# Message passing on sorted buckets: more groups scattered in pairs, column heads fetched sooner, other buffer counts

## The chip, the cores and the metric

The kernel runs on one core of one Trainium2 chip. Its time is the device time of one execution in microseconds (us). Three runs of the kernel before are given, and one profiled execution, whose trace shows every instruction of the five engines: PE (matrix products), DVE (vector operations), ACT (activations), POOL (here it issues the indirect DMAs) and SP (it issues the plain DMAs).

## The reference

There are 12,500 nodes with 128 features each and 400,000 edges, each with a source `src`, a destination `dst`, 20 attributes `f` and a weight. The edges are sorted by `dst`, while `src` is random.

```python
h   = relu(layernorm(x))
hh  = h @ W_in2f.T
Wij = (smu(f_ij @ W_f1.T + b_f1) @ W_f2.T + b_f2) * rcut_ij[:, None]
x_ij = hh[dst] * Wij
agg = segment_sum(x_ij, src, 12500)
out = x + smu(agg @ W_o1.T + b_o1) @ W_o2.T + b_o2
```

Here `smu` is a smooth bend that the kernel computes with a Gelu and a linear part. Each edge makes a message of 128 numbers, and the messages are summed by `src`, which comes in no order.

## The kernel before

**Tiles, groups, epochs.** The edges form 3125 tiles of 128. Four tiles are a *group* (782 of them), two groups a *super-group*. The 391 super-groups are divided into ten *epochs* (`PARTS`). The nodes are divided into 98 *bins* of 128.

**Scatter.** For each edge of a group the kernel computes the bin of its source and its rank among the edges of the epoch that fall into this bin (`mark_bins`, `bins`, `count`, `read`, `number`: one-hot marks, prefix sums on PE, a maximum on DVE). That gives a row number in a buffer in device memory with a fixed number of rows per bin and epoch (`CAP`). POOL then sends the group's message tile there with indirect DMAs (`scatter_rows`, L1069), one for each tile of 128 rows. A row has 129 numbers: the message and the place of the source in its bin. Three buffers are used in turn by the epochs.

**Sum.** In the epoch that follows, SP reads the buffer back (`fetch`, four chunks ahead), DVE turns the places into one-hot matrices `se` (`choose`, L1117), and PE multiplies rows by them and sums over a bin (`add`, L1130). DVE adds the result of four bins at a time to `agg` (L1144). `chores` and `parts` spread this work evenly over the groups of the epoch.

**The order.** All of PE, DVE, ACT and SP is written out by hand in one loop over positions `p` (L1637). At each position the steps of several groups are issued: the sends of this group, the products of the next, the gathers of the one after, the counts of the next but one. `seq` is the order of the groups. The groups of the last two epochs (23 super-groups, `s >= EARLY`) are interleaved into epochs 1 to 4: they are computed early, already multiplied by the first output weight, and stored in `kept_rows`; their bins are counted at that time too. They are scattered only in the *last stretch*, after epoch 7 (L1819 to L1851), where `refill` reads them back four groups ahead through SP.

**Pairs.** In some groups, tiles 2 and 3 are sent together with tiles 0 and 1. Rows of the two halves that have the same bin are put side by side, so that one indirect DMA writes two rows per partition. A paired group needs two sends in place of four, and one tile of *leftovers* (rows that found no partner) is sent as a fifth tile by a later group, its *host*. For this PE turns the keys of the group (`spread_keys`, L813), DVE compares them (`match`, L822, with the number of matches added up in `met`), PE ranks the rows without a partner (`rank_left`, L832), DVE builds the placing matrix (`place_left`, L839), PE permutes (`permute`, L859), ACT takes the result out (`take_pairs`, L870 and L871; leftovers go into `lt`, three buffers), and DVE makes the leftovers' bins (`number_left`, L849). The host counts them as one tile more (L707, L708, L750, L804). Which group is paired is decided in L539 to L550: after `EVERY` positions since the last pair (4 in epoch 0, 3 in the others), from position 80 on, and not in the last ten groups of an epoch; a group at least five positions behind a pair becomes its host. The host is looked for first. In the last stretch, every third group (`LATE_EVERY`) is paired, and its leftovers are sent by themselves three groups later.

**Column heads.** The columns `dst` and `src` are read in seven heads of 512 tiles (`head_of`). Their steps stand in a timetable in *slots* (three per position). `fetched` issues the two loads on SP, and `based`, DVE's first use (L410), comes 2.5 slots later; for heads whose time is before `known` (the first three of the six in the timetable) the loads are moved 9 slots forward (L1443).

**Buffers.** Messages `ms` rotate through nine buffers, halves `cd` through two, the rows read back `rw` through four.

Of the kernel before, what the change touches and what calls it, by code (L numbers as in the profile page):

```python
# [20 lines left out]
P = 128  # L21
# [10 lines left out]
WIN = 42  # L32
PARTS = (60, 58, 58, 58, 47, 37, 27, 23, 16, 7)
EVERY = (4, 3, 3, 3, 3, 3, 3, 3)
UNPAIRED = 10
MOST_PAIRS = 224
FIRST_PAIRED = 80
LATE_EVERY = 3
WIDER = 0.17
SENT_LAST = 2  # L40
BUFS = 3
SIGMA = 4.95
ROW = P + 1
# [7 lines left out]
def gnn_kernel(  # L51
# [46 lines left out]
    for a, n in eps_of:  # L98
        last_groups = UNPAIRED / (SUP // GRP)
        paired = n - last_groups if 0 < len(CAP) < len(eps_of) - 1 else 0  # L100
        if not CAP:
            paired = max(0, n - last_groups - FIRST_PAIRED / (SUP // GRP))
        every = LATE_EVERY if len(CAP) >= len(eps_of) - SENT_LAST else EVERY[len(CAP)]
# [241 lines left out]
    with tc.tile_pool(name="ld", bufs=4) as ld, \  # L345
            tc.tile_pool(name="edge", bufs=2) as edge, \
            tc.tile_pool(name="cnt", bufs=3) as cnt, \
            tc.tile_pool(name="msg", bufs=9) as msg, \
            tc.tile_pool(name="row", bufs=4) as rowp, \
# [116 lines left out]
        dsf, ssf = front[:, 2, :FEW], front[:, 3, :FEW]  # L466
        met = const.tile([P, 2 * MOST_PAIRS], F16, name="met")
        h_first = met.bitcast(BF)[:, :3 * D].rearrange("p (b k d) -> p b k d", b=1, k=3)
        nc.scalar.dma_start(x_sb[:, 0:1, :], bin_rows(x, 0, 1))
# [69 lines left out]
        for p, g in enumerate(seq):  # L539
            if g // PER >= EARLY:  # L540
                continue
            since_pair += 1
            if wanting and p >= wanting[0][0] + 5:
                host[g] = wanting.pop(0)[1]
                assert epoch[g // PER] == epoch[host[g] // PER]
            elif (since_pair >= (math.floor, math.ceil)[len(paired) % 2](EVERY[epoch[g // PER]])
                  and (epoch[g // PER] or p >= FIRST_PAIRED) and seq[p - 1] // PER < EARLY and g + UNPAIRED < ends_of[epoch[g // PER]]):
                paired[g] = len(paired)
                wanting.append((p, g))
                since_pair = 0  # L550
        assert not wanting
# [3 lines left out]
        assert 2 * len(pair_no) <= met.shape[1]  # L555
        late_keys = const.tile([P, len(late_pairs), GRP], F32, name="late_keys")
        so_end = const.tile([P, NB], F16, name="so_end")
# [251 lines left out]
        def spread_keys(g):  # L809

            kt = ps1.tile([P, GRP * P], F32, name="pt")
            for j in range(2):
                nc.tensor.transpose(kt[:, j * P:(j + 1) * P], keys_of[g][:, j:j + 1].to_broadcast([P, P]), ident)  # L813
            matched[g] = kt

        def match(g):

            kt, key = matched[g], keys_of.pop(g)
            pp = edge.tile([P, 6 * P], F32, name="mt", bufs=2)
            o = 2 * pair_no[g]  # L820
            for i in range(2):
                nc.vector.scalar_tensor_tensor(pp[:, i * 2 * P:(i + 1) * 2 * P].rearrange("p (j e) -> p j e", j=2),  # L822
                                               kt[:, :2 * P].rearrange("p (j e) -> p j e", j=2), key[:, 2 + i:3 + i],
                                               onesb.unsqueeze(1).to_broadcast([P, 2, P]),
                                               op0=ALU.is_equal, op1=ALU.mult, accum_out=met[:, o + i:o + i + 1])
            matched[g] = (kt, pp)

        def rank_left(g):

            kt, i = matched[g][0], 2 * pair_no[g]  # L830
            at_ = kt[:, 2 * P:2 * P + 2]
            nc.tensor.matmul(at_, tri, met[:, i:i + 2], start=True, stop=False, skip_group_check=True)  # L832
            nc.tensor.matmul(at_[:, 1:2], ones_h, met[:, i:i + 1], start=False, stop=True, skip_group_check=True)

# [16 lines left out]
        def permute(g):  # L851
# [9 lines left out]
            matched[g] = po  # L861

        def take_pairs(g):
# [546 lines left out]
        def due(t, f):  # L1410
            timetable.append((t, len(timetable), f))
# [361 lines left out]
        def flag_formed():  # L1773

            few_met = ps1.tile([P, GRP * P], F32, name="pc")[:, :2 * len(pair_no)]
            nc.tensor.matmul(few_met, ones_h, met[:, :2 * len(pair_no)], start=True, stop=True)
            sums = mv.rearrange("p b s -> p (b s)")[:, :len(pair_no)]
            nc.vector.tensor_reduce(sums, few_met.rearrange("p (g i) -> p g i", i=2), op=ALU.add, axis=AX.X)
            least_met = const.tile([P, 1], F32, name="least_met")
            nc.vector.tensor_reduce(least_met, sums, op=ALU.min, axis=AX.X)  # L1780
            i = 4 + 2 * EPOCHS
# [292 lines left out]
```

## Time and profile before

| | |
|---|---|
| runs shown | 3869.15, 3873.28, 3874.53 us (median 3873.28) |
| profiled execution | 3877.55 us, its span 3875.5 us |
| PE, DVE, ACT, POOL busy | 85%, 79%, 73%, 75% of the span |
| mean busy share of the 16 DMA engines | 63.4% for SP's queue, 17.6% for POOL's |
| memory traffic | 904.79 MB, mean 233 GB/s |

How to read the rows: a group's row gives the line of the kernel, the engine, the operation, out<-in by the program's names, the shapes and the count; then the busy time in us and the mean of one in ns; then the idle time of the engine just before these instructions, with what ended most of it. A row of waits names the engine and line that waited, what for, the total in us, how often, and the longest. A row of the timeline begins with the start and the duration in us. A row of a window gives its bounds and length, then the busy time (and the number) for PE, weight load, DVE, ACT, POOL, and the granted clock, DMA share and GB/s; where it was asked for one line's instructions, only the engine of that line is shown. The busy share of PE is that of matmuls whose ends are modelled.

The epochs can be told apart in the trace by counting the message products (L1002 and L992, one per group that is not kept): epoch 1 begins at about 618 us, epoch 2 at 1202, epoch 3 at 1750, epoch 4 at 2305, epoch 5 at 2750, epoch 6 at 3094, epoch 7 at 3365, and the last stretch at about 3566. POOL's last send begins at 3815.7 us.

### The profile page before, as it was taken

To read this page: it belongs to the slowest core of one execution; us is meant where nothing else is said; L and a number is where in the kernel's file an instruction comes from. 1 tells how busy PE (TensorE), PEld (TensorE's weight loads), DVE (VectorE), ACT (ScalarE), POOL (GpSimd) and SP (SyncE) were. 2 spreads that over 40 slices of the span, in tenths; PEclk is the share of its full clock that TensorE was granted. 3 is DMA by queue.
4 is the path that set the end of the run, shared out by engine and by line. 5 is a ranking of instruction groups with operands and counts; after the bars stand their busy time and mean duration, and the time that the engine had idled before them with its cause. 6 is when DMAs were issued, how large, how long until landed. Compare 5 with 4: busy or idle time off the path is not lost.

```text
span 3875.5 us, 89505 instructions
## 1 busy us (share of the span) xinstructions
PE 3289.4 (85%) x27505; PEld 2851.7 (74%) x27505; DVE 3066.3 (79%) x8171; ACT 2831.6 (73%) x8043; POOL 2889.8 (75%) x2977
## 2 busy tenths in 40 slices
PE   8766677888888888899888889899989988999667
PEld 4345555777777777788777778788888878888557
DVE  7887786778777888888888888888888877888557
ACT  7776666778777888788888888788877876776102
POOL 6777777777677777777777777777777777777776
PEclk9988898999999999999999999999999999999889
DMA  5887878889897877788887878878888888887988
GB/s 155 225 238 222 235 222 236 243 242 257 249 264 222 230 220 222 225 238 230 227 225 221 239 213 249 235 230 234 246 234 237 245 233 226 237 237 213 285 258 241
DMA packets 663934, 904.79 MB, mean 233 GB/s; under 512 B 180372, under 2 KB 463128, under 8 KB 663322
## 3 DMA queue, kind: packets, MB, share of 16 engines
q1 hardware_dynamic: 556025, 666.99, 63.4%
q0 software_dynamic: 100112, 219.73, 17.6%
q10 hardware_dynamic: 7312, 12.29, 0.9%
q8 instruction: 223, 3.65, 0.4%
q14 instruction: 262, 2.14, 0.2%
HBM read 500.66 MB, written 398.03 MB: 232 GB/s over the span
## 4 chain that ended last, share of the span: by engine, by line
PE 31%; DVE 17%; DMA 17%; issue 8%; ACT 8%; POOL 7%; SPq 1%; DVEq 0%; ACTq 0%; POOLq 0%
DMA buf<-ms,ix 11%; PE pg L1130 10%; POOL buf L1072 7%; PE pw L970 6%; PE pt L859 5%; PE pc L735 3%; ACT hg L945 3%; DVE se L1117 3%; DVE pc L779 2%; DMA rbc<-rel_dram 2%; DVE mt L822 2%; DVE ms L1002 2%; PE ph L926 2%; DVE eo L654 2%; DMA buf<-lt,ix 2%
## 5 line engine op out<-in xcount | busy, mean ns | idle before, releaser
L1072 POOL DMA_INDIRECT buf<-ms,ix x2578 | 2506.5, 972 | 846.6 <-issue 566.1
L1130 PE MATMUL pg<-se,rw 128*128 128x128 f32 x8036 | 1171.4, 285 | 116.6 <-DVE se L1117 52.7
L1130 PEld LDWEIGHTS pg<-se,rw 128*128 128x128 f32 x8036 | 1042.0, 195 | 162.6 <-DVE agg L1144 56.6
L945 ACT ACTIVATE hg<-ph,w_sb 128x128 f32<-128x128 f32 x2784 | 788.6, 364 | 491.3 <-PE ph L926 468.0
L970 PE MATMUL pw<-w_f,ge 128*128 128x128 f32 x5568 | 778.3, 284 | 12.7 <-DVE ms L1002 7.6
L970 PEld LDWEIGHTS pw<-w_f,ge 128*128 128x128 f32 x5568 | 701.1, 197 | 31.1 <-ACT ge L898 8.0
L1117 DVE TENSOR_TENSOR se<-irow_ps,rw 128x1536 f32<-128x1536 f32 (+1 forms) x345 | 587.4, 1703 | 94.3 <-DMA rw<-buf 74.6
L779 DVE TENSOR_REDUCE pc<-pc 128x4 f32<-128x392 f32 (+1 forms) x782 | 463.6, 593 | 154.5 <-PE pc L735 150.4
L617 ACT ACTIVATE oh<-rbc,nrow 128x512 bf16<-128x512 uint8 x724 | 538.2, 743 | 38.9 <-DMA rbc<-rel_dram 38.9
L618 ACT ACTIVATE oh<-oh,onesb 128x512 bf16<-128x512 bf16 x742 | 535.3, 721 | 24.2
L1002 DVE TENSOR_TENSOR ms<-pw,hg 128x512 f32<-128x512 f32 x513 | 351.4, 685 | 128.5 <-PE pw L972 42.6
L859 PE MATMUL pt<-cd,mt 128*128 128x129 f32 (+1 forms) x2304 | 311.2, 287 | 82.4 <-DVE at L839 76.1
L735 PE MATMUL pc<-eo,tri 128*128 128x392 f16 x782 | 266.9, 341 | 110.2 <-DVE ix L801 88.4
L859 PEld LDWEIGHTS pt<-cd,mt 128*128 128x128 f32 x2304 | 286.5, 199 | 96.5 <-issue 49.6
L926 PE MATMUL ph<-hw,oh 126*128 126x128 bf16 x2784 | 280.7, 224 | 24.0 <-ACT hg L945 24.0
L898 ACT ACTIVATE ge<-pu 128x512 f32<-128x512 f32 x452 | 275.6, 610 | 18.7 <-PE pu L890 16.7
L735 PE MATMUL pc<-so,ones_h 128*128 128x392 f16 (+1 forms) x965 | 281.4, 314 | 0.0
L972 PE MATMUL pw<-wls,f 128*128 128x128 bf16 x2784 | 273.7, 222 | 0.0
L735 PEld LDWEIGHTS <-ones_h 128*128 128x128 f16 x1554 | 154.9, 100 | 149.1 <-issue 32.7
L926 PEld LDWEIGHTS <-oh 126*128 126x128 bf16 x2784 | 220.0, 100 | 45.6 <-issue 28.1
L654 DVE TENSOR_TENSOR eo<-irow_ps,ed 128x784 f16<-128x784 f16 x391 | 218.2, 558 | 37.2 <-ACT ed L644 34.2
L1072 POOL DMA_INDIRECT buf<-lt,ix x192 | 185.9, 968 | 65.5 <-issue 28.7
(339 smaller groups left out, 5088.7 us busy)
## 6 DMA issues: line engine op xcount, KB each, us to landing
rw<-buf SPq DMA_DIRECT2D x292, 774.0 KB
f<-f_parts SPq DMA_DIRECT2D x370, 240.0 KB
buf<-zero SPq DMA_DIRECT2D x146, 387.0 KB
rbc<-rel_dram SPq DMA_DIRECT2D x389, 128.0 KB
buf<-ms,ix POOLq DMA_INDIRECT x2578
f_parts<-hs SPq DMA_DIRECT2D x104, 360.0 KB
rw<-buf SPq DMA_DIRECT2D x49, 645.0 KB
f_parts<-hs SPq DMA_DIRECT2D x106, 240.0 KB
```

The lines of the kernel that those rows point to most:

```text
L617: nc.scalar.activation(oh, loaded[s][1][:, o:o + n], AF.Abs, bias=pneg if s < FEW // SUP else nrow)
L618: nc.scalar.activation(oh, oh, AF.Relu, scale=-1.0, bias=onesb[:, 0:1])
L735: nc.tensor.matmul(to, by, of, start=start, stop=stop, skip_group_check=True)
L779: nc.vector.tensor_reduce(sl[:, :n], pc[:, :n], op=ALU.max, axis=AX.X)
L859: nc.tensor.matmul(po[:, j * (ROW + 1):j * (ROW + 1) + w], pp[:, o:o + P], cd[:, i, :w], start=(i == 0), stop=(i == 1))
L926: nc.tensor.matmul(ph[:, j * P:(j + 1) * P], oh[:3 * WIN, a:a + P], hw[:3 * WIN, g % PER, :], start=True, stop=True)
L945: nc.scalar.activation(hg[:, j * P:(j + 1) * P], rows_of[g][:, j * P:(j + 1) * P], AF.Copy, scale=w_sb[:, t + j:t + j + 1])
L970: nc.tensor.matmul(pw[:, a:a + P], ge[:, a:a + P], w_f2, start=(a == 0), stop=False, skip_group_check=True)
L1002: nc.vector.tensor_tensor(ms[:, :n, 0:P], pw.rearrange("p (j f) -> p j f", f=P)[:, :n], hg.rearrange("p (j f) -> p j f", f=P)[:, :n], op=A ...
L1072: i = nc.gpsimd.indirect_dma_start(out=(wide if g in host or g in pair_no else bufs)[k][:, :], out_offset=bass.IndirectOffsetOnAxis(ap=ix, ...
L1117: nc.vector.tensor_tensor(se[:, a:a + n], own.unsqueeze(1).to_broadcast([P, n, P]), rows_in[c][:, a:a + n, P:P + 1].to_broadcast([P, n, P] ...
L1130: nc.tensor.matmul(pgs[0][:, g, :], rows_in[c][:, o, 0:P], sel[c][:, o, :], start=(q == 0), stop=(q == Q[k] - 1))
```

## The change

- **More pairs.** The distance is 3 in epoch 0 and, in the others, 2 and 3 in turn (`EVERY` 2.5, rounded down and up alternately); pairs begin at position 50; a pair is looked for before a host, so that hosts come at a distance of 5 to 8. In the last stretch two groups of three are paired. `SIGMA` is 4.6, and epoch 0 has 59 super-groups and epoch 7 has 24; the bucket sizes `CAP` come out as before. The sums of matches no longer fit into `met` alone and go on in the unused `down`; `late_keys` lies in `mv`.
- **Destinations sooner.** The loads of all six heads in the timetable are moved 9 slots forward.
- **Six buffers for leftovers.** `lt` has six buffers; messages `ms` have eight in place of nine. Late leftovers lie in two `ge` tiles, late halves `cd` in part in `oh`. There are four spill places per buffer instead of two.
- **Kept rows five groups ahead.** `refill` runs five groups ahead in place of four. In the last stretch keys are turned in another bank (`pw`), and `place_of_left` comes before `number_left`.

```diff
-PARTS = (60, 58, 58, 58, 47, 37, 27, 23, 16, 7)
-EVERY = (4, 3, 3, 3, 3, 3, 3, 3)
+PARTS = (59, 58, 58, 58, 47, 37, 27, 24, 16, 7)
+EVERY = (3,) + (2.5,) * 7
-FIRST_PAIRED = 80
-LATE_EVERY = 3
+FIRST_PAIRED = 50
+LATE_OF = 2, 3
+LATE_FREE = 6
-SIGMA = 4.95
+SIGMA = 4.6
...
-    SPILLS = 2
+    SPILLS = 4
...
-            tc.tile_pool(name="msg", bufs=9) as msg, \
+            tc.tile_pool(name="msg", bufs=8) as msg, \
...
-            if wanting and p >= wanting[0][0] + 5:
-                host[g] = wanting.pop(0)[1]
-            elif (since_pair >= (math.floor, math.ceil)[len(paired) % 2](EVERY[epoch[g // PER]])
+            if (since_pair >= (math.floor, math.ceil)[len(paired) % 2](EVERY[k]) and (k or p >= FIRST_PAIRED)
+                    and seq[p - 1] // PER < EARLY and g + UNPAIRED < ends_of[k]):
                 paired[g] = len(paired)
                 wanting.append((p, g))
                 since_pair = 0
+            elif wanting and p >= wanting[0][0] + 5:
+                host[g] = wanting.pop(0)[1]
...
-        late_pairs = list(range(EARLY * PER + LATE_EVERY - 1, LATE_END - 3, LATE_EVERY))
+        late_pairs = [g for g in range(EARLY * PER + 2, LATE_END - 3) if (g - EARLY * PER) % LATE_OF[1] >= LATE_OF[1] - LATE_OF[0]]
...
-            kt = ps1.tile([P, GRP * P], F32, name="pt")
+            kt = ps1.tile([P, GRP * P], F32, name="pt" if g in paired else "pw")
...
-            lt = cnt.tile([P, ROW + 1], F32, name="lt", bufs=3)
+            lt = cnt.tile([P, ROW + 1], F32, name="lt", bufs=6) if g in paired else late_left(g)
...
-            due(t + 0.5 - (SOONER if t < known else 0), stages.pop(0))
+            due(t + 0.5 - SOONER, stages.pop(0))
...
-                    cd = apart_of[g] = msg.tile([P, 2, ROW + 1], F32, name="cd", bufs=2)
+                    if late_pairs.index(g) % 5 < 3:
+                        cd = edge.tile([P, SUP * P], BF, name="oh", bufs=3).bitcast(F32)[:, :2 * (ROW + 1)]
+                        cd = apart_of[g] = cd.rearrange("p (j r) -> p j r", j=2)
+                    else:
+                        cd = apart_of[g] = msg.tile([P, 2, ROW + 1], F32, name="cd", bufs=2)
...
-            few_met = ps1.tile([P, GRP * P], F32, name="pc")[:, :2 * len(pair_no)]
-            nc.tensor.matmul(few_met, ones_h, met[:, :2 * len(pair_no)], start=True, stop=True)
-            nc.vector.tensor_reduce(sums, few_met.rearrange("p (g i) -> p g i", i=2), op=ALU.add, axis=AX.X)
+            for a, b, at_ in ((0, n, met), (n, len(pair_no), more_met)):
+                by_pair = at_[:, :2 * (b - a)].rearrange("p (g i) -> p g i", i=2)
+                for i in range(2):
+                    nc.tensor.matmul(few_met[:, a:b], ones_h, by_pair[:, :, i], start=(i == 0), stop=(i == 1))
...
-        for g in range(g1, g1 + 4):
+        AHEAD_OF = 5
+        for g in range(g1, g1 + AHEAD_OF):
             refill(g)
...
-            refill(g + 4)
+            refill(g + AHEAD_OF)
...
+            if g - 1 in late_pairs:
+                place_of_left(g - 1)
             if g in late_pairs:
                 number_left(g)
                 count_left(g)
             parts(hi)
-            if g - 1 in late_pairs:
-                place_of_left(g - 1)
```

More of the change, by code (lines that the diff above doesn't have):

```diff
@@ L102, in gnn_kernel @@
             paired = max(0, n - last_groups - FIRST_PAIRED / (SUP // GRP))
-        every = LATE_EVERY if len(CAP) >= len(eps_of) - SENT_LAST else EVERY[len(CAP)]
+        late_one = len(CAP) >= len(eps_of) - SENT_LAST
+        every = LATE_OF[1] / LATE_OF[0] if late_one else EVERY[len(CAP)]
+        if late_one and paired:
+            paired = n - LATE_FREE / (SUP // GRP)
         mean = (n + WIDER * paired / every) * SUP * P * P / N
@@ L466, in gnn_kernel @@
         dsf, ssf = front[:, 2, :FEW], front[:, 3, :FEW]
[L467 to L468 removed]
+        met = const.tile([P, 3 * D], F16, name="met")
+        h_first = met.bitcast(BF).rearrange("p (b k d) -> p b k d", b=1, k=3)
         nc.scalar.dma_start(x_sb[:, 0:1, :], bin_rows(x, 0, 1))
@@ L542, in gnn_kernel @@
             since_pair += 1
-            if wanting and p >= wanting[0][0] + 5:
-                host[g] = wanting.pop(0)[1]
-                assert epoch[g // PER] == epoch[host[g] // PER]
-            elif (since_pair >= (math.floor, math.ceil)[len(paired) % 2](EVERY[epoch[g // PER]])
-                  and (epoch[g // PER] or p >= FIRST_PAIRED) and seq[p - 1] // PER < EARLY and g + UNPAIRED < ends_of[epoch[g // PER]]):
+            k = epoch[g // PER]
+            if (since_pair >= (math.floor, math.ceil)[len(paired) % 2](EVERY[k]) and (k or p >= FIRST_PAIRED)
+                    and seq[p - 1] // PER < EARLY and g + UNPAIRED < ends_of[k]):
                 paired[g] = len(paired)
@@ L824, in match @@
                                                onesb.unsqueeze(1).to_broadcast([P, 2, P]),
[L825 removed]
+                                               op0=ALU.is_equal, op1=ALU.mult, accum_out=met_of(g, i))
             matched[g] = (kt, pp)
         def rank_left(g):
[L830 removed]
+            kt = matched[g][0]
             at_ = kt[:, 2 * P:2 * P + 2]
[L832 to L833 removed]
+            nc.tensor.matmul(at_, tri, met_of(g, 0, 2), start=True, stop=False, skip_group_check=True)
+            nc.tensor.matmul(at_[:, 1:2], ones_h, met_of(g, 0), start=False, stop=True, skip_group_check=True)
         def place_left(g):
```

26 lines of the change are left out of this document (20 added, 6 removed).

## The prediction

> **What bounds the kernel now.** I read the page's busy times first. No engine looks full there, POOL least of all, so I took POOL's rows and then its instructions in order of time:
>
> ```profile
> span 3875.5 us, 89505 instructions
> PE 3289.4 (85%) x27505; PEld 2851.7 (74%) x27505; DVE 3066.3 (79%) x8171; ACT 2831.6 (73%) x8043; POOL 2889.8 (75%) x2977
> L1072 POOL DMA_INDIRECT buf<-ms,ix x2578 | 2506.5, 972 | 846.6 <-issue 566.1
> L1072 POOL DMA_INDIRECT buf<-lt,ix x192 | 185.9, 968 | 65.5 <-issue 28.7
> L1072 POOL DMA_INDIRECT buf<-ms,ix_kept x163 | 156.7, 962 | 49.7 <-issue 46.0 <-DMA buf<-ms,ix_kept 1.8 <-DMA hic<-in_x 0.3
> 3499.18 0.96 POOL L1072 DMA_INDIRECT buf<-lt,ix  x1 [0.30 <-issue]
> 3500.44 0.96 POOL L1072 DMA_INDIRECT buf<-ms,ix  x1 [0.30 <-issue]
> ```
>
> A send occupies POOL for 0.96 us and is followed by 0.30 us in which nothing is waited for: one per 1.26 us, whether it carries one row per partition (lt) or two. The three rows hold 2933 sends, 3705 us at 1.263 each, while their busy and idle time together are 3811 us. POOL is 97% full with sends; about 105 us are starvation. It is not starved everywhere:
>
> ```profile
> L1072 POOL DMA_INDIRECT buf<-ms,ix x695 | 676.7, 974 | 244.0 <-issue 164.9 <-ACT ms L1052 20.6 <-ACT hg L945 14.1
> L1072 POOL DMA_INDIRECT buf<-lt,ix x63 | 61.2, 971 | 19.6 <-issue 10.4 <-DVE ms L992 1.5 <-DVE pc L779 1.2
> ...
> L1072 POOL DMA_INDIRECT buf<-ms,ix x289 | 279.2, 966 | 88.2 <-issue 61.3 <-DMA buf<-ms,ix 4.6 <-ACT oh L617 3.1
> L1072 POOL DMA_INDIRECT buf<-lt,ix x27 | 26.1, 967 | 8.2 <-issue 2.7 <-DVE so L701 0.9 <-DVE ix L801 0.6
> ```
>
> The first two rows are 700 to 1700 us (epochs 1 and 2): 1001.5 us for 758 sends, 1.32 each. The last two are 1800 to 2200 us (epoch 3): 401.7 for 316, 1.27 each. So in epochs 1 and 2 POOL runs out of work now and then: PE, DVE and ACT, which make the messages, are no faster than POOL. I call them the makers. How far they are ahead at the end of epoch 7:
>
> ```profile
> 3565.85 0.68 DVE L1002 TENSOR_TENSOR ms<-pw,hg 128x512 f32<-128x512 f32 x1
> ...
> 3599.18 0.96 POOL L1072 DMA_INDIRECT buf<-ms,ix_kept  x1 [0.30 <-issue]
> ```
>
> The last message of epoch 7 is made at 3566.5; POOL begins the kept rows at 3599.2, so that message's four sends began at 3594.1: a reserve of 27.6 us. Both sides bind, in turn. A pair relieves POOL by one send and loads the makers; which weighs more decides.
>
> **What a pair costs the makers.** Walking the pairing rule through the order of groups gives, for epochs 0 to 7, 8, 34, 33, 33, 27, 21, 15 and 12 pairs now (183) and 19, 42, 41, 41, 33, 25, 18 and 15 after (234); in the last stretch 9 become 17. That is 59 sends fewer, 74.5 us of POOL. Each early pair adds, beside a plain group (its host's extra work included):
>
> ```profile
> L822 DVE SCALAR_TENSOR_TENSOR mt<-pt,key,onesb 128x256 f32<-128x256 f32 x366 | 161.7, 479 | 21.1 <-PE pt L813 19.9
> L840 DVE TENSOR_TENSOR mt<-irow_ps,at 128x256 f32<-128x256 f32 x192 | 81.5, 424 | 6.6
> L707 DVE TENSOR_SCALAR el<-mv,lat 128x98 f16<-128x98 f32 x183 | 53.8, 294 | 0.3
> L708 DVE TENSOR_TENSOR so<-so,el 128x98 f16<-128x98 f16 x183 | 39.0, 213 | 6.3
> L859 PE MATMUL pt<-cd,mt 128*128 128x129 f32 (+1 forms) x2304 | 311.2, 287 | 82.4 <-DVE at L839 76.1
> ```
>
> DVE: two of the first row (0.96) and one of each of the next three (0.93), 1.9 us, and, as an estimate from these, some 0.7 for four or five smaller ones: 2.6. PE: 311.2/192 = 1.6 us of permuting and under 1 us of turning and counting. Some of this falls into idle time, so the price is better measured. The last ten groups of an epoch have no pairs. In the same windows I counted L654 (one per two groups) and L840 (one per pair); epoch 2 first, then epoch 5, L654 ahead of L840 in each:
>
> ```profile
> 1215.00:1695.00 480.00, 30.73 (x55) 0.98 0.79 225
> 1695.00:1750.00 55.00, 3.92 (x7) 0.97 0.85 236
> 1215.00:1695.00 480.00, 13.15 (x31) 0.98 0.79 225
> 1695.00:1750.00 55.00, 0.42 (x1) 0.97 0.85 236
> ...
> 2760.00:3036.00 276.00, 15.69 (x28) 0.98 0.84 233
> 3036.00:3094.00 58.00, 3.90 (x7) 1.00 0.92 257
> 2760.00:3036.00 276.00, 8.06 (x19) 0.98 0.84 233
> 3036.00:3094.00 58.00, 0.42 (x1) 1.00 0.92 257
> ...
> 3390.00:3520.00 130.00, 7.83 (x14) 0.97 0.87 239
> 3530.00:3565.00 35.00, 2.23 (x4) 1.00 0.75 207
> 3390.00:3520.00 130.00, 3.82 (x9) 0.97 0.87 239
> 3530.00:3565.00 35.00, 0.00 (x0) 1.00 0.75 207
> ```
>
> With a for a group and c for a pair: epoch 2, 110a + 31c = 480 and 14a + c = 55, so c = 2.07; epoch 5, 56a + 19c = 276 and 14a + c = 58, so c = 2.93; epoch 7, 28a + 9c = 130 and 8a = 35, so c = 0.83. I take 2.07, since 24 of the 51 new early pairs lie in epochs 1 to 3, which resemble epoch 2, and keep 0.83 and 2.93 as ends. 51 × 2.07 = +106 us for the makers (42 to 149).
>
> The Trainium skill (Perfetto Trace Analysis, Identifying the Most-Contended Engine) judges TensorE's headroom by weight-load share, not matmul share; the page of the profile has 74% against 85%. By it the pair's PE work would find more room than I grant, and c would go to its low end, the first rival below.
>
> **Destinations sooner.** Between 320 and 500 us:
>
> ```profile
> DVE base_i L410 <- DMA rw<-in_dst_col: 37.9, 3, 15.0
> POOL buf L1072 <- DVE ix L804: 6.9, 1, 6.9
> ```
>
> The fourth to sixth column heads are fetched 2.5 slots before use; now 11.5. Three slots make a group, so the two loads of each head go onto SP's queue three groups sooner, ahead of the loads of edges, destinations and windows that those groups issue. Three groups are 618/120 × 3 = 15 us, the longest of the waits. I take 35 of the 37.9 away (0 to 38). The head takes an rw buffer of four that much sooner; if it isn't free, SP waits and every load behind it is late.
>
> **Buffers.** The makers' waits for places that POOL still holds:
>
> ```profile
> ACT lt L871 <- DMA buf<-lt,ix: 17.7, 11, 5.6
> ACT ms L1052 <- DMA buf<-ms,ix: 10.3, 6, 6.2
> ACT ms L1050 <- DMA buf<-ms,ix: 5.9, 7, 1.6
> DVE ms L1002 <- DMA buf<-ms,ix: 21.1, 21, 2.5
> ```
>
> Six leftover buffers end the first (17.7); the others (37.3) shrink because POOL, with fewer sends, frees messages sooner. Eight message buffers in place of nine work against that by one group, four sends, 5 us of reserve. I take all 55 away (0 to 55).
>
> **Costs of nothing.** Hosts yield to pairs and come at a distance of six mostly: the leftover has longer to land its count, same instructions. The sums of met need four small matmuls for one and one DVE reduction fewer, while PE waits for epoch 8's rows. Late leftovers lie in ge, late halves in oh: both unused there until the output begins, after POOL's last send; late keys are turned in bank pw, free there too. place_of_left goes ahead of number_left on DVE, two short operations:
>
> ```profile
> 3565.00:3817.00 252.00, 171.92 (x1306) 153.71 (x1305) 148.65 (x235) 21.02 (x50) 191.21 (x199) 0.88 0.83 264
> DVE se L1117 <- DMA rw<-buf: 61.2, 13, 26.2
> SPq L1771 <- DMA buf<-ms,ix_kept: 11.9, 5, 3.5
> ...
> L1536 DVE TENSOR_SCALAR drow<-pcol 128x1 f32<-128x1 f32 x20 | 1.3, 138 | 0.0
> ```
>
> In the last stretch DVE is busy 149 of 252 us and PE 172, each with waits for rows still in flight, which cover eight more late pairs (8 × 5 us over all engines). Without that cover they cost up to 8 × 2.07 = 17. Reading kept rows five groups ahead with eight buffers makes SP wait for the sends of three groups back rather than five; the row fetches for the sums queue behind that wait and DVE waits for those. They are asked for four chunks ahead, so I put it at 0, with the 11.9 above once more as the upper end. Four spill places per epoch instead of two repeat the 20 operations of the last row: 1.3 us at most, in epoch 0 before the makers have anything to catch up. Bucket sizes come out the same, so reads and clears stay; one super-group moves from epoch 0 to 7 with its work. A pair writes 640 rows for 512, in fewer sends, beside the other transfers.
>
> **The sum.** The makers' end of epoch 7 moves by −35 + 106 − 55 = +16, to 3582. The reserve was 27.6; fed by the ten unpaired groups alone, (4 × 1.263 − 3.85) × 10 = 12 us (a is 3.78 from epoch 2's equations, 3.93 from epoch 5's) and a start near 1, it becomes 13. So POOL ends epoch 7 at +16 − 15 = +1. The last stretch is POOL's: 8 × 1.263 = −10. The 59 us after the last send stay. Together −9: the profiled run (3877.55 us, 2 more than its span) would be 3868; the median of the runs shown, 3873.28, lies 4 below it, so 3864.
>
> **Rivals.**
> - *The pairs' work fits into idle time.* c at 0.83 takes 51 × 1.24 = 63 off: 3801; POOL alone allows 3873 − 74.5 = 3799, so some 3805. For it: PE, DVE and ACT each idle 15 to 27%. Against: epoch 2's and 5's rows.
> - *The pairs cost the makers 2.93 each* (slower). Place: the chain of turning keys (PE), matching (DVE), ranking (PE), placing (DVE) and permuting (PE), which at a distance of two uses the one bank pt in every group. Price 51 × 0.86 = +44: 3908. It decides from c = 2.07 + 9/51 = 2.25 on. For it: PE's 76.1 us of waits for at above; against: epochs 0 to 3, where most pairs go, have fewer sums per group.
> - *Destinations sooner does not do what it says:* the loads wait for something other than their place. +35: 3899. Against: the waits are the only ones of their kind, the first three heads already go sooner and have none.
> - *DVE sets the time by its share.* If DVE stayed at its 79%, 59 × 2.6 = 153 us more would be 194 us more: 4067. Against: POOL's spacing. The section of the Trainium skill named above ranks DVE, ACT and POOL by occupancy; by that rule DVE (79%) would be the most contended, ahead of POOL (75%); POOL's 1.26 us spacing does not agree.
>
> **Chances.** Forecast 0.44 (its own range 3840 to 3890), the rivals 0.22, 0.23, 0.08, 0.03. A measurement here can tell 0.2%, 8 us, from no change. Faster: 0.24 of the forecast, 0.22, 0.02 of the second rival, 0.48. Same: 0.11, 0.04 and 0.02, 0.17. Slower: 0.35. The range runs from near POOL's floor, 3805, to 3902, most of the second rival.
>
> **What would show it.** Right: the three waits at L410 gone; waits for lt gone; 2874 sends, still 1.26 us apart where fed; POOL's idle time beyond 0.30 per send up from 105 us towards 150 in epochs 1 to 6, with PE and DVE busier there; the reserve at the end of epoch 7 about halved. The first rival would show as idle time that does not grow; the second as longer waits at L859 and its neighbours and a later end of epoch 7. What would make me wrong most: a price per pair away from 2.07.

## The result and the profile after

The changed kernel takes 3926.68 us (median of four runs, 3924.54 to 3929.99) against 3872.11 us (3869.15 to 3874.53) before: ratio 1.0142 with a 95% interval of 1.0124 to 1.0160. It is slower by some 55 us, where 3864 us was forecast, and it lies outside the range of 3805 to 3902. The profiled executions, on which the working below rests, are 47 us apart: 3924.54 us (span 3922.8) and 3877.55 us (span 3875.5).

The page of the kernel after: the span, the busy times, and POOL's rows (count | busy, mean ns | idle before, and what ended it).

```profile
span 3922.8 us, 92185 instructions
PE 3349.1 (85%) x28254; PEld 2939.6 (75%) x28570; DVE 3178.1 (81%) x8771; ACT 2888.3 (74%) x8332; POOL 2841.5 (72%) x2918
L1095 POOL DMA_INDIRECT buf<-ms,ix x2476 | 2412.6, 974 | 847.0 <-issue 576.4 <-DMA buf<-ms,ix 37.9 <-ACT ms L1075 29.0
L1095 POOL DMA_INDIRECT buf<-lt,ix x234 | 227.8, 974 | 141.3 <-DVE ix L816 84.3 <-issue 22.0 <-DVE eo L666 5.2
L1095 POOL DMA_INDIRECT buf<-ms,ix_kept x147 | 143.7, 978 | 63.0 <-issue 42.6 <-ACT ge L894 12.4 <-DMA ms<-kept_rows 4.5
L1095 POOL DMA_INDIRECT buf<-ge,ix x17 | 16.7, 982 | 5.9 <-issue 3.4 <-DVE lat L860 0.9 <-DVE ix L1845 0.7
```

The 2874 sends that were worked out are there (2476 + 234 + 147 + 17), each still 0.97 us long with 0.30 behind it. POOL works 48 us less than before. But it waits more: the time between the beginnings of two sends, as far as it exceeds 1.30 us, adds up to 202 us after and 91 before. For epoch 0, epochs 1 to 4, epochs 5 to 7 and the last stretch, in this order, it is 28, 149, 4 and 21 us after, and 27, 57, 7 and 0.5 before. The largest new wait is for the index of a host's fifth send. Its rows among the waits (engine, line, what for: total in us, times, longest), after and then before:

```profile
POOL buf L1095 <- DVE ix L816: 88.6, 61, 5.1
```

```profile
POOL buf L1072 <- DVE ix L804: 11.9, 16, 6.9
```

POOL sends a host's leftovers ahead of the host's own messages, and their index is made shortly before those messages. So the wait says that POOL has nothing else left to send: it has caught up with the makers, 61 times for 16.

Where the time went is read from POOL's sends by stretch. The stretches begin with the first send of epoch 1, the first of epoch 5 and the first kept row. Columns: bounds, length, POOL's busy time and sends, clock, DMA share, GB/s. After:

```profile
622.00:2817.00 2195.00, 1568.54 (x1612) 0.97 0.80 230
2817.00:3634.70 817.70, 621.96 (x642) 0.98 0.83 234
3634.70:3864.00 229.30, 160.40 (x164) 0.91 0.90 272
```

Before:

```profile
644.00:2778.00 2134.00, 1592.54 (x1642) 0.97 0.83 235
2778.00:3599.10 821.10, 624.82 (x644) 0.96 0.82 230
3599.10:3817.00 217.90, 165.37 (x172) 0.89 0.89 285
```

- **Epochs 1 to 4**: 30 sends fewer, 61 us longer. Per send 1.362 us after and 1.300 before. POOL is starved here: the makers set the time. Since epoch 1 begins 22 us sooner, epoch 5 begins 39 us later.
- **Epochs 5 to 7**: two sends fewer (ten more pairs, and one super-group with eight sends more), 3.4 us shorter. Per send 1.274 and 1.275 us. POOL sets the time here, in both kernels.
- **Last stretch**: eight sends fewer, 11.4 us longer. Per send 1.398 and 1.267 us: POOL is starved where it was not.

39 − 3.4 + 11.4 = 47 us, which is the whole difference of the spans. So the pairs cost time exactly where POOL was already waiting, and the sends that they save count only in epochs 5 to 7, where there are few of them.

The makers' side of epochs 1 to 4, epoch by epoch: the windows go from the first message of an epoch to the first of the next, with busy time and count of PE, weight load, DVE, ACT and POOL. After:

```profile
606.00:1200.00 594.00, 499.46 (x4285) 445.82 (x4339) 450.70 (x1281) 467.03 (x1382) 412.21 (x424) 0.95 0.85 243
1755.00:2332.00 577.00, 506.12 (x4405) 451.68 (x4463) 470.38 (x1316) 477.88 (x1370) 420.12 (x433) 0.98 0.78 221
2332.00:2790.00 458.00, 417.25 (x3733) 379.38 (x3779) 391.28 (x1064) 374.44 (x1078) 326.29 (x336) 0.99 0.80 230
```

Before, the same three epochs (1, 3 and 4):

```profile
618.00:1202.00 584.00, 492.72 (x4194) 433.38 (x4193) 434.83 (x1202) 460.11 (x1340) 427.93 (x441) 0.94 0.87 248
1750.00:2305.00 555.00, 495.52 (x4318) 437.12 (x4317) 454.31 (x1236) 469.34 (x1329) 421.97 (x437) 0.98 0.80 227
2305.00:2750.00 445.00, 407.80 (x3663) 366.99 (x3661) 379.31 (x1002) 367.73 (x1042) 333.29 (x345) 0.99 0.83 237
```

With eight, eight and six pairs more, these epochs take 10, 22 and 13 us longer; epoch 2, with eight more, takes 7 longer. Over the four it is 52 us for 30 pairs, 1.7 each. DVE's busy time grows by 16, 16 and 12 us, PE's by 7, 11 and 9.

The reserve at the end of epoch 7, from the last message (DVE) and the first kept send (POOL), kernel after:

```profile
3598.16 0.68 DVE L1025 TENSOR_TENSOR ms<-pw,hg 128x512 f32<-128x512 f32 x1
...
3634.73 0.96 POOL L1095 DMA_INDIRECT buf<-ms,ix_kept  x1 [0.30 <-issue]
```

The message is made at 3598.8, its four sends began at 3634.7 − 4 × 1.26 = 3629.7: 30.8 us, against 27.6 before. It was not halved.

### The profile page after: what moved, and what is told of

Same layout as the page of the kernel before. It is cut to its first block, busy times and chain, and to the rows that moved or that the text cites. A ratio compares the mean times of both kernels' runs of the same rounds, so it can differ in the third digit from the quotient of the medians.

```text
span 3922.8 us, 92185 instructions
## 1 busy us (share of the span) xinstructions
PE 3349.1 (85%) x28254; PEld 2939.6 (75%) x28570; DVE 3178.1 (81%) x8771; ACT 2888.3 (74%) x8332; POOL 2841.5 (72%) x2918
## 3 DMA queue, kind: packets, MB, share of 16 engines
q0 software_dynamic: 100112, 223.62, 17.7%
## 5 line engine op out<-in xcount | busy, mean ns | idle before, releaser
L1095 POOL DMA_INDIRECT buf<-ms,ix x2476 | 2412.6, 974 | 847.0 <-issue 576.4
L630 ACT ACTIVATE oh<-oh,onesb 128x512 bf16<-128x512 bf16 x743 | 536.0, 721 | 24.1
L870 PE MATMUL pt<-cd,mt 128*128 128x129 f32 (+1 forms) x2880 | 373.8, 280 | 55.5 <-DVE at L850 49.7
L1025 DVE TENSOR_TENSOR ms<-pw,hg 128x512 f32<-128x512 f32 x462 | 316.3, 685 | 111.8 <-PE pw L995 36.2
L870 PEld LDWEIGHTS pt<-cd,mt 128*128 128x128 f32 x2880 | 346.4, 194 | 67.3 <-issue 38.8
L1095 POOL DMA_INDIRECT buf<-lt,ix x234 | 227.8, 974 | 141.3 <-DVE ix L816 84.3
L833 DVE SCALAR_TENSOR_TENSOR mt<-pt,key,onesb 128x256 f32<-128x256 f32 x468 | 207.0, 480 | 52.1 <-PE pt L825 49.6
```

What stands on the lines that cost most here:

```text
L630: nc.scalar.activation(oh, oh, AF.Relu, scale=-1.0, bias=onesb[:, 0:1])
L870: nc.tensor.matmul(po[:, j * (ROW + 1):j * (ROW + 1) + w], pp[:, o:o + P], cd[:, i, :w], start=(i == 0), stop=(i == 1))
L1025: nc.vector.tensor_tensor(ms[:, :n, 0:P], pw.rearrange("p (j f) -> p j f", f=P)[:, :n], hg.rearrange("p (j f) -> p j f", f=P)[:, :n], op=A ...
L1095: i = nc.gpsimd.indirect_dma_start(out=(wide if g in host or g in pair_no else bufs)[k][:, :], out_offset=bass.IndirectOffsetOnAxis(ap=ix, ...
```

## Experiments

A ratio is always to the kernel before, run on the same chip. On three of the chips the kernel before took 5914 to 5979 us instead of 3865 to 3872; their runs are told apart, at the end.

**Old distances in the changed kernel.** The pairs of the epochs go back to 189 (133 in place of 157 in epochs 1 to 4); everything else of the change stays.

```diff
-EVERY = (3,) + (2.5,) * 7
-FIRST_PAIRED = 50
+EVERY = (4,) + (3,) * 7
+FIRST_PAIRED = 80
```

> The changed kernel with the old pairing of epochs 0 to 7 alone (distance 4 in epoch 0 from position 80, 3 elsewhere; 183 early pairs), all else as changed. If the added early pairs cost the makers about 2 us each in epochs 1 to 4 (theory), POOL begins the last stretch about 35 us sooner than the changed kernel's 3635 us, and the time is 3880 to 3895. If the eight message buffers are the cause (rival), the time stays above 3910 and the reserve at the ends of the epochs stays lower than before.

Measured: 3899.40 us, ratio 1.0093 (1.0077 to 1.0110), about 19 us better than the change as a whole. That is 4 us above what the theory allowed and well below the rival's 3910. POOL begins the last stretch at 3608, 27 us sooner. The makers take 2151 us for epochs 1 to 4 where the changed kernel takes 2184: 33 us for 24 pairs, 1.4 each. Most of the way back to the kernel before is still missing.

**Late thirds in the changed kernel.** One group of three is paired in the last stretch, as before.

```diff
-LATE_OF = 2, 3
+LATE_OF = 1, 3
```

> The changed kernel with every third group paired in the last stretch as before (9 late pairs, not 17), all else as changed. If the late pairs at two of three make POOL wait in the last stretch (theory), POOL's waits of 2 to 4 us between 3680 and 3760 us go, the stretch of 229 us falls to about 217, and the time is 3910 to 3917. If reading five groups ahead with eight buffers makes POOL wait (rival), the waits stay and the time is 3927 or more.

Measured: 3918.30 us, ratio 1.0135 (1.0118 to 1.0152), which isn't told apart from 1.0142. The trace says more. POOL's rows from 3638 to 3858 us of this kernel, its last stretch:

```profile
L1095 POOL DMA_INDIRECT buf<-ms,ix_kept x163 | 158.4, 972 | 49.7 <-issue 44.8 <-DMA buf<-ms,ix_kept 3.0 <-ACT ge L894 0.6
L1095 POOL DMA_INDIRECT buf<-ge,ix x9 | 8.9, 987 | 2.7 <-issue 1.8 <-ACT agg L1181 0.6 <-ACT oh L1795 0.3
```

172 sends in 219.4 us, 1.28 each; with two of three, 164 in 229. The waits for L894 (a late leftover taken out by ACT) fall from 12.4 us to 0.6. So the eight additional late pairs lose some 10 us instead of gaining 10, and reading five groups ahead hardly makes POOL wait.

**Both at once.**

```diff
-EVERY = (3,) + (2.5,) * 7
-FIRST_PAIRED = 50
-LATE_OF = 2, 3
+EVERY = (4,) + (3,) * 7
+FIRST_PAIRED = 80
+LATE_OF = 1, 3
```

> Both undone: old pairing everywhere; what remains of the change is the sooner column loads, six leftover buffers, eight message buffers and kept rows read five groups ahead. Theory: the two effects add, 3865 to 3880, no slower than the kernel before. Rival (buffers): 3895 or more.

Measured: 3890.26 us, ratio 1.0057 (1.0038 to 1.0075). Beside the kernel with old distances alone this is 9 us better, the last stretch 220 us instead of 226; so the late thirds do show in the time here. Beside the one with late thirds alone it is 28 us better: that is what the added early pairs cost. The two effects do add, but the time lies between the theory's 3880 and the rival's 3895. With the pairs nearly those of before, the kernel is still 0.57% slower than before.

**Destinations sooner, alone**, in the kernel before.

```diff
-            due(t + 0.5 - (SOONER if t < known else 0), stages.pop(0))
+            due(t + 0.5 - SOONER, stages.pop(0))
```

> The kernel before with the sooner column loads alone. The three waits at L410 (37.9 us) go. Theory: epoch 1's first message comes some 25 us sooner but POOL, which still has its sends, lets only 5 to 10 us of it through: 3862 to 3868. Rival (the makers set the time throughout): 3840 to 3850. Second rival (an rw buffer that is not free makes SP wait): 3872 or more.

Measured: 3863.12 us, ratio 0.9993 (0.9984 to 1.0003). Waits of this kernel between 300 and 604 us (engine, line, what for: total, times, longest), and one of the whole trace:

```profile
ACT oh L617 <- DMA rbc<-rel_dram: 48.7, 20, 6.8
...
DVE base_i L410 <- DMA rw<-in_dst_col: 1.6, 1, 1.6
```

The answering rows of the kernel before, 300 to 618 us:

```profile
DVE base_i L410 <- DMA rw<-in_dst_col: 37.9, 3, 15.0
ACT oh L617 <- DMA rbc<-rel_dram: 20.8, 8, 6.1
```

The waits for the column heads go, as the change means it. But the loads of relative destinations, behind the heads on SP's queue or beside them, are now waited for 28 us longer. The makers begin epoch 1 at 603.5 instead of 618.3, POOL at 637 instead of 644: of 37.9 us, 15 reach the makers and 7 reach POOL, and no difference in the time can be measured. Part of that may be the difference from one execution to another: the kernel of the next experiment, whose heads are those of before and are waited for 38.1 us, begins epoch 1 at 609.1.

**Eight message buffers, alone**, in the kernel before.

```diff
-            tc.tile_pool(name="msg", bufs=9) as msg, \
+            tc.tile_pool(name="msg", bufs=8) as msg, \
```

> The kernel before with eight message buffers, again, since on the chip of the first try PE stood still so often that the kernel before took 5979 us. Theory: the ninth message buffer was worth 0.4 to 0.7% (15 to 27 us). Rival (what was left of the loss without the added pairs comes from the order of pairs and hosts): within 0.15% of the kernel before.

Measured: 3868.97 us, ratio 1.0000 (0.9989 to 1.0011). In the kernel before, the ninth buffer is worth nothing that can be measured.

**Old pairs, with the old buffers as well** (nine for messages, three for leftovers, in the kernel "both").

```diff
-            tc.tile_pool(name="msg", bufs=8) as msg, \
+            tc.tile_pool(name="msg", bufs=9) as msg, \
...
-            lt = cnt.tile([P, ROW + 1], F32, name="lt", bufs=6) if g in paired else late_left(g)
+            lt = cnt.tile([P, ROW + 1], F32, name="lt", bufs=3) if g in paired else late_left(g)
```

> The changed kernel with old pairing, nine message and three leftover buffers, again. Theory (the message buffer): within 0.15% of the kernel before. Rival (the order of pairs and hosts): still 0.4% slower or more.

Measured: 3885.14 us, ratio 1.0043 (1.0029 to 1.0057), not to be told from 1.0057. The buffers are not what remains, or at most a small part of it. POOL's stretches in this kernel and, behind them, in the one with destinations sooner alone (epochs 1 to 4, then 5 to 7):

```profile
628.00:2764.00 2136.00, 1585.85 (x1635) 0.97 0.83 234
2764.00:3592.00 828.00, 629.34 (x651) 0.97 0.81 230
```

```profile
637.00:2761.00 2124.00, 1598.17 (x1641) 0.97 0.82 235
2761.00:3581.70 820.70, 624.05 (x644) 0.97 0.81 230
```

The super-group moved to epoch 7 is seven more sends and 7.3 us in POOL's stretch. Epoch 0, one super-group shorter, gives 9 us back to POOL and 9 to the makers; but in epochs 1 to 4 it is 12 us longer, with six more pairs there (hosts yield to pairs). That would fit 1.8 to 2 us a pair; it is read off one execution of each (3872.99 us, the shortest of its six, and 3861.73), and no run has the moved super-group or the order of hosts alone on a chip of the usual speed. So the 17 to 22 us that remain are not settled: of some 55 us, the added early pairs explain 28 and the late ones 9.

**Fewer pairs where the makers set the time.** In the kernel before with destinations sooner: every 3.5 groups in epochs 1 to 4, 113 pairs there for 127.

```diff
-EVERY = (4, 3, 3, 3, 3, 3, 3, 3)
+EVERY = (4, 3.5, 3.5, 3.5, 3.5, 3, 3, 3)
```

> The kernel before with sooner columns and pairs at distances of 3 and 4 in turn in epochs 1 to 4, again. On the chip with the slow PE this was 2.5% faster than the kernel before, as it must be where the makers set the time. Here: 10 to 25 us faster than the kernel before if the makers set the time in epochs 1 to 4; 15 to 25 us slower if POOL does; both in turn: 3 to 15 us slower.

Measured: 3860.61 us, ratio 0.9984 (0.9974 to 0.9993): the opposite edit to the change, and slightly faster than the kernel before. It is 7 us, in none of the three ranges that were expected, and it is not told apart from destinations sooner alone (0.9993, 0.9984 to 1.0003). POOL's stretch of epochs 1 to 4:

```profile
636.00:2760.00 2124.00, 1608.87 (x1657) 0.97 0.83 235
```

That is 16 sends more than with destinations sooner alone, in the same 2124 us. POOL's idle time beyond 1.30 us per send is 56 us, the least so far.

**The same with six leftover buffers and eight for messages**, and a distance of 2.5 in epochs 5 to 7.

```diff
-EVERY = (4, 3, 3, 3, 3, 3, 3, 3)
+EVERY = (4, 3.5, 3.5, 3.5, 3.5, 2.5, 2.5, 2.5)
-SIGMA = 4.95
+SIGMA = 4.6
-            tc.tile_pool(name="msg", bufs=9) as msg, \
+            tc.tile_pool(name="msg", bufs=8) as msg, \
-            lt = cnt.tile([P, ROW + 1], F32, name="lt", bufs=3)
+            lt = cnt.tile([P, ROW + 1], F32, name="lt", bufs=6)
```

> The same, and pairs at distances of 2 and 3 in turn in epochs 5 to 7, with six leftover and eight message buffers. In the changed kernel POOL had a reserve of 19 to 31 us at the ends of these epochs, so the makers can carry more pairs there. Theory: 10 pairs fewer sends in a stretch that POOL sets, 12 us faster than the kernel with distances 3 and 4 alone. Rival (the makers set the time there too at this density, 2.9 us a pair): 10 to 20 us slower than it.

Measured: 3854.20 us, ratio 0.9961 (0.9949 to 0.9973): faster than the kernel before, and 6 us faster than the previous one, half of what the theory said. The bucket sizes are those of before. The shorter distance did not do what it was meant to: the rule looks for a host first, and so epochs 5 to 7 got one pair more (49 for 48), not a dozen. What sets this kernel off from the previous one is thus that pair and the buffers, of which the eight message buffers alone showed nothing; why it is faster is open. Its POOL rows and its longest waits for places (the profiled execution, 3864.20 us, was the longest of its eight):

```profile
L1072 POOL DMA_INDIRECT buf<-ms,ix x2604 | 2539.0, 975 | 823.2 <-issue 551.9 <-DMA buf<-ms,ix 46.4 <-ACT hg L945 24.7
L1072 POOL DMA_INDIRECT buf<-lt,ix x179 | 174.0, 972 | 55.1 <-issue 27.4 <-DVE pc L779 3.5 <-DVE so L701 2.4
```

```profile
DVE ms L1002 <- DMA buf<-ms,ix: 124.9, 55, 7.2
ACT ms L1052 <- DMA buf<-ms,ix: 74.9, 37, 6.4
ACT ms L1050 <- DMA buf<-ms,ix: 69.8, 40, 5.7
```

The fastest kernel has by far the longest waits for places, 270 us in these three rows against 37 before. A maker that waits for a place is ahead of POOL. POOL was fed as well here as in the previous kernel (61 us of idle time beyond 1.30 us per send, against 56), so these waits cost little or nothing.

**On the three slower chips.** The kernel with eight message buffers, its first lines, its clock, and two of its waits:

```profile
span 5955.5 us, 89265 instructions
PE 3860.0 (65%) x27191; PEld 3314.8 (56%) x27505; DVE 3094.6 (52%) x8171; ACT 2872.8 (48%) x8043; POOL 2888.4 (49%) x2977
```

```profile
core 0: 5955.5 us, clock 0.803
```

```profile
ACT hg L945 <- remote: 1077.2, 179, 12.2
DVE pc L779 <- remote: 741.3, 123, 12.0
```

POOL is 49% busy, and its sends come at 2.08 us each in epochs 1 to 4, 2.07 in epochs 5 to 7 and 1.81 in the last stretch: the makers set the time throughout, and the number of sends sets it nowhere. What was run there says what an edit costs the makers on such a chip, and little about the other chips.

Eight message buffers, and six leftover buffers with them (the latter as in the diff above, kernel before):

> The kernel before with eight message buffers in place of nine, nothing else. Undoing all the added pairs left the changed kernel 0.57% slower than the kernel before although its columns come sooner. Theory: the ninth message buffer was worth it, because the makers then stand still for places more often in epochs 1 to 4: 0.4 to 0.7% slower, 15 to 27 us, more waits of messages (ms) for POOL's sends than the 37 us of before. Rival (the order of pairs and hosts costs it): within 0.15% of the kernel before.

> The kernel before with eight message buffers and six leftover buffers. The waits of lt (17.7 us) go. Theory (message buffers matter in epochs 1 to 4, leftover buffers in epochs 5 and 6, where POOL sets the time anyway): as slow as with eight message buffers alone, within 5 us. Rival (leftover buffers give back what the message buffer takes): within 0.1% of the kernel before.

Measured: 0.9996 (0.9968 to 1.0024) and 0.9986 (0.9956 to 1.0016). Neither shows.

Old pairs with old buffers, and fewer pairs in epochs 1 to 4:

> The changed kernel with old pairing everywhere, and nine message and three leftover buffers: left are the sooner columns, pairs looked for before hosts (189 early pairs), four spill places, and reading five groups ahead. Theory (the message buffer): the 0.57% by which the same kernel with eight and six was slower go, within 0.15% of the kernel before. Rival (the order of pairs and hosts, or reading ahead): still 0.4% slower or more.

> The kernel before with the sooner columns, and pairs at distances of 3 and 4 in turn in epochs 1 to 4: some 18 pairs fewer there. If a pair costs the makers 2 us and the makers set the time in epochs 1 to 4, it is 10 to 25 us faster than the kernel with the sooner columns alone (3838 to 3853 on a chip where the kernel before takes 3865). If POOL sets the time there, its 18 sends more cost 23 us: 3880 to 3890. If both bind in turn, as I read the trace of before, the second outweighs: 3868 to 3882.

Measured: 0.9858 (0.9820 to 0.9897) and 0.9753 (0.9699 to 0.9808). With the makers as the only limit, destinations sooner and 14 pairs fewer are worth 2.5%.

The order of hosts and pairs: pairs first in the kernel before (every 3.5 groups in epochs 6 and 7), and hosts first in the changed kernel with old pairs.

```diff
-            if wanting and p >= wanting[0][0] + 5:
-                host[g] = wanting.pop(0)[1]
...
-            elif (since_pair >= (math.floor, math.ceil)[len(paired) % 2](EVERY[epoch[g // PER]])
+            if (since_pair >= (math.floor, math.ceil)[len(paired) % 2](EVERY[epoch[g // PER]])
...
+            elif wanting and p >= wanting[0][0] + 5:
+                host[g] = wanting.pop(0)[1]
```

> The kernel before with pairs looked for before hosts (epochs 6 and 7 at distances of 3 and 4 in turn, so that the sums of matches still fit). If this order is what is left of the loss: 0.4% slower than the kernel before or more, with longer epochs 2 to 4. If not: within 0.15%.

> The changed kernel with the old distances, every third group in the last stretch, and hosts looked for first as before: left are the sooner columns, six and eight buffers, four spill places, 59 and 24 super-groups, and reading five groups ahead. If the order is the cause: within 0.15% of the kernel before, like the sooner columns alone (0.07% faster). If not: still 0.4% slower or more.

Measured: 0.9911 (0.9884 to 0.9938) and 1.0008 (0.9988 to 1.0029); the second once more on another chip of this kind 0.9990 (0.9963 to 1.0018). The kernel with pairs first is the faster one here, though it has 185 pairs, six more than before in epochs 1 to 4; the second has 183, and destinations sooner too, and gains nothing. So on these chips the number of pairs alone does not say which kernel is faster. It speaks against the order of hosts as what remains in the kernel "both", but for makers on chips of this kind only.

Two variants of the kernel of 0.9961: with three groups' distance in epochs 1 to 4 again, and with more pairs in epoch 0:

```diff
-EVERY = (4, 3.5, 3.5, 3.5, 3.5, 2.5, 2.5, 2.5)
+EVERY = (4, 3, 3, 3, 3, 2.5, 2.5, 2.5)
...
-EVERY = (4, 3.5, 3.5, 3.5, 3.5, 2.5, 2.5, 2.5)
-FIRST_PAIRED = 80
+EVERY = (3, 3.5, 3.5, 3.5, 3.5, 2.5, 2.5, 2.5)
+FIRST_PAIRED = 50
```

> The kernel before with sooner columns, six and eight buffers, and distances of 2 and 3 in turn in epochs 5 to 7 alone (3 in epochs 1 to 4). Theory: where POOL sets the time the added pairs pay, about 10 us faster than the sooner columns alone, which were 0.07% faster than the kernel before. Rival: the makers set the time there, the same or slower than the kernel before.

> The best kernel so far (distances 3 and 4 in turn in epochs 1 to 4, 2 and 3 in epochs 5 to 7, which was 0.39% faster than the kernel before) with distance 3 from position 50 on in epoch 0 as well. POOL's reserve at the end of epoch 0 was 31 us there. Theory: some 11 sends less, 10 us faster again, 0.6 to 0.7% faster than the kernel before. Rival: the makers lose in epoch 0 what POOL gains, no faster than 0.4%.

Measured: 0.9884 (0.9852 to 0.9917) and 0.9734 (0.9693 to 0.9775), the second again 0.9754 (0.9703 to 0.9805). The first has nearly the pairs of before (184; hosts come first in its rule too), and destinations sooner and the other buffers. But these do not explain its 1.2%: the changed kernel with old pairs and hosts first (1.0008, on the same chip) has them too. Of the 85 us between the two, 71 lie in epochs 5 to 7 (1286 us from the first message to the last, against 1357), where the first kernel has one super-group fewer and its pairs stand at other distances; the cause is open. The second has 14 pairs fewer in epochs 1 to 4 and 12 more in epoch 0, and gains another 1.5%. Its traces show where: epochs 1 to 4 take the makers 3227 us instead of 3388, but epoch 1 begins at 855 and 863 us instead of 804. So the 12 pairs in epoch 0 do cost the makers time, 4 to 5 us each on these chips. Neither was run on a chip of the usual speed.

## Why the prediction was wrong, point by point

Three steps failed: waits for buffers were counted as time that the makers win, the reserve was to take up 15 us, and the late pairs were to gain 10 us. What bounds, and nearly the price of a pair, were right.

**What bounds: right, but not used to the end.** Epochs 1 to 4 belong to the makers and epochs 5 to 7 to POOL; the prediction had the row for the first (1.32 us per send) and the reserve of 27.6 us for the second. It then took the end of epoch 7 as a time of the makers, to which every pair adds and from which a reserve is spent. By stretch the makers begin epoch 1 12 us sooner, take 52 us longer for epochs 1 to 4, and 7 us less for epochs 5 to 7, with ten pairs and a super-group more: the added pairs cost about what was worked out in epochs 1 to 4, and nothing in epochs 5 to 7.

**The price of a pair: nearly right.** 2.07 us was taken. The makers pay 52 us for 30 pairs in epochs 1 to 4, 1.7 each; if the 8 us of waits for places that went there (below) are counted in, it is 2.0. The ten profiles on chips of the usual speed agree: epochs 1 to 4 take the makers 2113 and 2128 us with 113 pairs, 2130 to 2139 with 127, 2141 to 2151 with 133, and 2184 and 2188 with 157, which is 1.5 a pair from end to end, though these kernels differ in other edits too. The second rival, 2.93 with longer waits at the permutation or its neighbours, had the sign of the result but not the price. The permutation's waits became shorter, and those of the matching for the turned keys longer; kernel after:

```profile
PE pt L870 <- DVE at L850: 49.7, 52, 2.3
```

```profile
L833 DVE SCALAR_TENSOR_TENSOR mt<-pt,key,onesb 128x256 f32<-128x256 f32 x468 | 207.0, 480 | 52.1 <-PE pt L825 49.6
```

They were 76.1 and 19.9 before. So the chain that the rival named does wait longer at one of its steps, by 30 us. The first rival, pairs that fit into idle time, falls for epochs 1 to 4, where they cost 1.7 us each. So headroom by weight-load share, which the prediction weighed (the Trainium skill, Perfetto Trace Analysis, Identifying the Most-Contended Engine), was no guide to the price: weight load is at 75% after, and the pairs still found no room there.

**Destinations sooner: the waits right, their worth wrong.** All three waits at L410 went, so the third rival falls, but at most 15 us reach the makers, not 35. The step's own warning, that loads behind the heads would be late, fits (waits for rel_dram, 20.8 to 48.7), though no run shows what those loads waited behind. In the changed kernel the makers begin epoch 1 12 us sooner, just what −35 + 23 gives. That is luck: three terms come to the same, at most 15 from the heads, the super-group that left epoch 0, which the sum left out, and 11 pairs.

**Buffers: the first step that failed.** All 55 us of waits for places were taken off the makers. Those for messages did not go (38.4 us in the rows below, 37.3 before). The leftovers' 17.7 us went, but they lay in epochs 5 to 7, where POOL sets the time; kernel before, 2750 to 3600 us:

```profile
ACT lt L871 <- DMA buf<-lt,ix: 17.7, 11, 5.6
```

There a maker's wait is free: with old pairs, epochs 5 to 7 take the makers 821 us with three leftover buffers, 24.1 us of them such waits, and 820 with six. In epochs 1 to 4, where it would have counted, the waits for places of L1002, L1050 and L1052 were 36.7 us before and are 28.4 after; the whole trace after has

```profile
DVE ms L1025 <- DMA buf<-ms,ix: 23.6, 20, 2.4
ACT ms L1073 <- DMA buf<-ms,ix: 9.7, 8, 2.2
ACT ms L1075 <- DMA buf<-ms,ix: 5.1, 4, 3.0
```

where 21.1, 5.9 and 10.3 stood. The makers' end of epoch 7 moved by +32, not +16. These 16 us are a balance: 55 from the buffers and 20 or more from the heads did not come, and the pairs of epochs 5 to 7 and the shorter epoch 0 give part of it back; no run splits it further. The prediction counted as a cost what is mostly a sign that the makers are ahead.

**The reserve: the second step that failed.** It was to fall from 27.6 to 13 and absorb 15 us. It is 30.8. In epochs 5 to 7 POOL needs 1.27 us a send in every kernel run on chips of the usual speed (817.7/642 after, 821.1/644 before, 828.0/651 with old pairs and old buffers, 820.7/644 with destinations sooner alone), so makers that are late at epoch 5 are ahead again by its end, and what was lost up to there is passed on whole. POOL began epoch 5 39 us late and the last stretch 35.5 us late. Working with ten unpaired groups alone, the step looked only at epoch 7's end. This is 18 us of the error.

**The last stretch: the third step that failed, in its sign.** −10 was forecast and +11.5 came, 21.5 us of the error. The cover was named (waits of DVE and PE for rows), and its lack put at up to 17. But the waits of DVE and PE for *summing* rows are no cover for POOL: a late pair must be turned, matched, placed, permuted and taken out before POOL has its rows, and POOL was fed without a gap before. It waits 12.4 us for leftovers (L894) and 4.5 for kept rows now. With thirds it is 219.4 and 220.1 us against 217.5: reading five ahead and the moved place_of_left cost 2 to 3 us at most, near the 0 that was taken.

**The sum.** Forecast +1 − 10 = −9 for the span, measured +35.5 + 11.5 = +47; 16 of the 56 us between are the makers', 18 the reserve's, 21.5 the last stretch's. The fourth rival (DVE by its share, 4067) is far off: DVE grew by 112 us, the time by 47.

## What to carry to other kernels

Where two sides take turns as the bound, work out a change stretch by stretch and pass the lead or the delay on: work moved from the one to the other is paid in the stretches where the receiver binds, and is saved only where the giver does. Read the giver's time per item in each stretch (here 1.27 us where POOL binds, 1.30 to 1.36 where it starves) before counting a single saving. Waits for free buffers were here the mark of a side that is ahead, and are no time to be won unless the same side binds just there.

## What was not expected of the hardware

On three chips the same kernel took 5914 to 5979 us instead of some 3870. There PE's granted clock was 0.80 instead of 0.95, PE was busy for 65% of the span instead of 85%, and ACT and DVE waited 1077 and 741 us for what the trace calls remote, up to 12 us at a time. Why is open, and so is whether the clock is a cause or follows from the standstill. Where POOL is fed, its sends begin 1.27 us apart there as elsewhere (the median of all).
